# Two sequences' projections as seven quarter products, four passes of two key heads, value pages by indirect transfers

## The chip, the cores and the metric

The kernel runs on one core of a Trainium2 chip, and the metric is the device time of one launch. The core has a matrix engine (TensorE, PE in the profile; PEld is its weight load), VectorE (DVE), ScalarE (ACT), GpSimd (POOL) and SyncE (SP, which here only issues transfers). Each takes its own instructions strictly in the order in which they stand in the program; semaphores order them against each other. Transfers are issued in the queues of SP, ACT and POOL and carried out by 16 DMA engines. Work is done in SBUF, a memory of 128 partitions; TensorE writes to PSUM, eight banks of 512 float32 numbers per partition.

## The reference

Eight sequences of 128 tokens with 512 features pass two residual blocks, all in float32. Block 0 multiplies by one of eight weight matrices per sequence, then by a base matrix with a bias, and adds a low-rank mixture of two of eight experts. Block 1 is attention over a paged cache, followed by a routed low-rank layer:

```python
q = _rope(_rmsnorm(x @ Wq.T, q_norm_w), pos)      # 32 query heads of 128
k = _rope(_rmsnorm(x @ Wk.T, k_norm_w), pos)      # 8 key heads
v = x @ Wv.T
kc = k_cache[block_table].reshape(bsz, 512, 8, 128)   # 16 pages of 32 tokens; vc alike
k_all = concat([kc, k]); v_all = concat([vc, v])      # 640 keys, each head serving 4 query heads
probs = softmax(where(valid, q @ k_all.T * SCALE, -1e30))
o = (probs @ v_all) @ Wo.T
out = x + ((o @ A_w.T).reshape(64, 8) * gate).reshape(512) @ B_w.T * 2
```

`gate` is a softmax over the 16 best of 64 experts. The output is the sequence after both blocks.

## The kernel before

The program is written out by hand: Python loops emit instructions, and each engine keeps the emitted order.

A first stage (lines 269 to 500) makes `x1`, the sequences after block 0, stores them to HBM and keeps them transposed in SBUF as `x1T`. It also loads the first weights of attention and makes the tables of cosines.

The attention stage works in *units*: one sequence and one key head with its four query heads, 64 in all. Units are listed by `units` (line 183) in two passes of four key heads (`GH` = 4): for each of the two halves of heads all eight sequences, and for each sequence four heads. A *step* is one sequence in one pass. `iteration(u)` (line 812) emits, for one value of `u`, pieces of five units:

- the transfers (SP): `gather` (149) loads the next step's key and value pages, one transfer for each page of `kt` and one of `vt`; `exchange_in(u-1)` (708) loads `qkb`, the blocks of rotated queries and keys of unit u+1, and `pT`, the transposed probabilities of unit u-1;
- then for each of four query heads: `scores(u, h)` (650), two matmuls against 512 cached and 128 own keys into a bank pair `s` (two pairs in turn); `mask_exp` (663), a masking pass on VectorE and an exponential on ScalarE; `normalize` of the head before (682), a reciprocal on VectorE and a multiplication on POOL; `blocks` of the head before that (687), a transpose of 32x32 blocks on VectorE into `pb`; and `output(u-2, h)` (751), one matmul of the output projection;
- after the four heads: `add_output(u-2)`, the last `normalize` and two `blocks`, and `exchange_out(u)` (695). That writes `pb`, and with it the queries and keys of unit u+2, to HBM in four transfers `px`, two on SP and two on ACT. Reading them back in another order completes the transpose;
- `project(u+3)`: four matmuls of 512 columns into bank `q` (queries) and four of 256 into bank `kv` (line 201, 214), then `norms` (227), five squares with sums and a copy of the values `vn` on ScalarE and a power on POOL, and `rotate(u+3)` (243) on VectorE;
- `heads_qk(u+1)` (718), a ScalarE copy that makes `qkT` out of `qkb`. The scores of unit u+1 read it;
- `values(u-1)` (727): five matmuls of `pT` with cached and own values, evicted by `evict_o` in the next iteration.

A unit's output of 128x512 is added to the step's sum `ya` on VectorE (line 770) after each unit; between the passes a sum goes to HBM and comes back (`y_d`, `load_y`).

The order within an engine matters for what follows. On ScalarE: four exponentials, two `px` issues (each waits for the last block transpose), five squares and the `vn` copy of unit u+3, the `qkT` copy of unit u+1, then `evict_o` of the next iteration. A transfer issue that waits holds up everything behind it in its engine's queue.

The last stage computes the routed layer. Four of its eight sequences are done within the last iterations (`LAST`, line 777 on), and four after them (`l2`, line 906).

Of the kernel before, what the change touches and what calls it, by code (L numbers as in the profile page):

```python
# [30 lines left out]
GH = HKV // 2  # L31
# [7 lines left out]
WARM = 22  # L39
# [14 lines left out]
def adaln_ffn_kernel(  # L54
# [5 lines left out]
    pages: bass.AP,  # L60
    lens: bass.AP,
# [32 lines left out]
    wp = ctx.enter_context(tc.tile_pool(name="wp", bufs=GH))  # L94
# [5 lines left out]
    pg = const.tile([1, B * NPP], I32, name="pg")  # L100

# [17 lines left out]
    lenf = const.tile([P, B], F32, name="lenf")  # L119
    cos = const.tile([P, B, D // 2], F32, name="cos")  # L120
    sin = const.tile([P, B, D // 2], F32, name="sin")

    x1T = keep.tile([P, B, NC, S], F32, name="x1T")
# [13 lines left out]
    def load_q(g, eng):  # L137
        t = wp.tile([P, NC, (REP + 2) * D], F32, tag="wqkv", name=f"wqkv_{g}")
        eng.dma_start(out=t, in_=wqkv[g].rearrange("(c p) n -> p c n", p=P))
        wq_t[g] = t  # L140

    def load_o(g, eng):
        t = wp.tile([P, REP, DM], F32, tag="wo", name=f"wo_{g}")
        eng.dma_start(out=t, in_=wo[g].rearrange("h p n -> p h n"))
        wo_t[g] = t
# [3 lines left out]
    def gather(step, first=0, end=NPP):  # L149
        hf, b = divmod(step, B)  # L150
        if first == 0:
            kv_t[step] = (
                kvp.tile([P, NPP, GH, PSIZE], F32, tag="kt", name=f"kt_{step}"),
                kvp.tile([P, LC, GH * D], F32, tag="vt", name=f"vt_{step}"),
            )
        kt, vt = kv_t[step]
        per = P // PSIZE
        for j in range(first, end):
# [6 lines left out]
            r0 = (j % per) * PSIZE  # L165
            nc.sync.dma_start(
                out=vt[r0 : r0 + PSIZE, j // per, :],
                in_=vc[hf, ds(page, 1)].rearrange("o p f -> p (o f)"),
# [14 lines left out]
    units = [(st, st // B * GH + j) for st in range(2 * B) for j in range(GH)]  # L183
    NU = len(units)
    q_t, kv_ps, rs_t, qk_t, vn_t, tab_t = {}, {}, {}, {}, {}, {}


    SWAP = (1, 3)
# [12 lines left out]
    def project_q(u):  # L201
        st, g = units[u]
        q = bank("o" if u in SWAP else "q", f"q_{u}")
        for c in range(NC):
            nc.tensor.matmul(  # L205
                out=q,
                lhsT=x1T[:, st % B, c, :],
                rhs=wq_t[g][:, c, : REP * D],
                start=(c == 0),
                stop=(c == NC - 1),  # L210
            )
        q_t[u] = q

    def project_kv(u):
        st, g = units[u]
        kv = bank("y" if u in SWAP else "kv", f"kv_{u}")[:, : 2 * D]
        for c in range(NC):
            nc.tensor.matmul(  # L218
                out=kv,
                lhsT=x1T[:, st % B, c, :],  # L220
                rhs=wq_t[g][:, c, REP * D :],
                start=(c == 0),
                stop=(c == NC - 1),
            )
        kv_ps[u] = kv

    def norms(u):

        q, kv = q_t[u], kv_ps[u]
        ss = pj.tile([P, NH], F32, tag="ss", name=f"ss_{u}", bufs=5)  # L230
        sq = pj.tile([P, D], F32, tag="sq", name=f"sq_{u}")
        for h in range(NH):
            src = q[:, h * D : (h + 1) * D] if h < REP else kv[:, :D]
            nc.scalar.activation(sq, src, AF.Square, accum_out=ss[:, h : h + 1])  # L234
        vn = pj.tile([P, D], F32, tag="vn", name=f"vn_{u}", bufs=5)
        nc.scalar.copy(vn, kv[:, D:])
        vn_t[u] = vn
        nc.gpsimd.tensor_scalar(ss, ss, 1.0 / D, EPS, ALU.mult, ALU.add)  # L238
# [4 lines left out]
    def rotate(u):  # L243

        st, g = units[u]
        q, kv, rs, tab = q_t.pop(u), kv_ps.pop(u), rs_t[u], tab_t[st]
        ca = pj.tile([P, NH, 2, D // 2], F32, tag="ca", name=f"ca_{u}")
        sa = pj.tile([P, NH, 2, D // 2], F32, tag="sa", name=f"sa_{u}")
        for i, o in enumerate((ca, sa)):
            ov = o.rearrange("p h t d -> p h (t d)")  # L250
            tv = tab[:, i].rearrange("p (i t) d -> p i (t d)", t=2)
            nc.vector.tensor_tensor(  # L252
                ov[:, :REP, :],
                q.rearrange("p (h d) -> p h d", h=REP),
                tv[:, 0:1, :].to_broadcast([P, REP, D]),
                ALU.mult,
            )
        for i, o in enumerate((ca, sa)):
# [3 lines left out]
                ov[:, REP, :], kv[:, :D], rs[:, REP:NH], tv[:, 1, :], ALU.mult, ALU.mult  # L262
# [6 lines left out]
    with ExitStack() as l0:  # L269
# [30 lines left out]
        homes = [(p2, "wt"), (p2, "wt"), (wp, "wo"), (kvp, "kt"), (kvp, "vt"), (wp, "wqkv")]  # L300
        wt_home = {}

        def l0_home(b):
            pool, tag = homes[b if b < 5 else b - 5 if b < 7 else 5]
            n = (REP + 2) * D if tag == "wqkv" else DM
            t = pool.tile([P, NC, n], F32, tag=tag, name=f"wt_{b}")
            wt_home[b] = t[:, :, :DM]

        for b in (0, 1, 2, 3, 4, 7):
            l0_home(b)  # L310
# [26 lines left out]
        )  # L337
        leni = w0p.tile([P, B], I32, name="leni")
# [102 lines left out]
        def l0_experts(b):  # L441
# [5 lines left out]
            state[b] = x1  # L447

        def l0_turn(b):
# [4 lines left out]
            nc.scalar.copy(x1T[:, b].rearrange("p c s -> p (c s)"), tp[:, :DM])  # L454
# [5 lines left out]
        for t in range(B):  # L460
# [4 lines left out]
            if t + 3 < B:  # L465
                if t + 3 in (5, 6):
                    l0_home(t + 3)
# [3 lines left out]
            if t >= 1:  # L471
                l0_experts(t - 1)
                if t in (3, 5, 7):
                    load_q((t - 3) // 2, nc.gpsimd)
# [6 lines left out]
            l0_base(t)  # L481
            if 1 <= t <= 4:
                l0_angles(t - 1)

        load_q(3, nc.gpsimd)
        for g in range(GH):
            load_o(g, nc.gpsimd)
        make_tables(0)
        project_q(0)
        l0_turn_low(B - 1)  # L490
        project_kv(0)
        norms(0)
        l0_experts(B - 1)
        l0_turn(B - 2)
        rotate(0)
        project_q(1)
        l0_turn(B - 1)
        project_kv(1)
        norms(1)
        rotate(1)  # L500
# [4 lines left out]
    def f_weights():  # L505
        awt = wp.tile([P, NC, (REP + 2) * D], F32, tag="wqkv", name="awt")
        nc.sync.dma_start(
            out=awt[:, :, :DM], in_=aw.rearrange("(c p) n -> p c n", p=P)
        )
        bwt = wp.tile([P, NC, (REP + 2) * D], F32, tag="wqkv", name="bwt")  # L510
        nc.sync.dma_start(
            out=bwt[:, :, :DM], in_=bw.rearrange("(c p) n -> p c n", p=P)
        )
        nc.sync.dma_start(
            out=awt[:RD, :, DM : DM + P], in_=wr.rearrange("r (c p) -> r c p", p=P)
        )
        nc.sync.dma_start(out=awt[:RD, 0, DM + P : DM + P + E1], in_=keys)
        fw_t["a"], fw_t["b"] = awt[:, :, :DM], bwt[:, :, :DM]
        fw_t["s"] = bwt[:, :, DM : DM + E1]
        fw_t["r"], fw_t["k"] = awt[:RD, :, DM : DM + P], awt[:RD, 0, DM + P : DM + P + E1]  # L520
# [10 lines left out]
    def f_turn(b, sb, psum):  # L531
        yb = ya_t.pop(B + b)
# [59 lines left out]

    ORDER = [B - 3, B - 2, 0, 1, 2, B - 1, 3, 4]
# [11 lines left out]
    with ExitStack() as l1:  # L605
# [145 lines left out]
        def output(u, h):  # L751
            st, g = units[u]
            if h == 0:
                y_t[u] = bank("y", f"y_{u}")
            nc.tensor.matmul(  # L755
                out=y_t[u],
                lhsT=oT_t[u][:, h, :],
                rhs=wo_t[g][:, h, :],
                start=(h == 0),
                stop=(h == REP - 1),  # L760
            )

        def add_output(u):
            st, g = units[u]
            y = y_t.pop(u)
            if g == 0:
                ya_t[st] = yp.tile([P, DM], F32, tag="ya", name=f"ya_{st}")
                nc.vector.tensor_copy(ya_t[st], y)
            else:
                nc.vector.tensor_tensor(ya_t[st], y, ya_t[st], ALU.add)  # L770
            if g % GH == GH - 1 and st < 2 * B - 3:
                nc.sync.dma_start(out=y_d[st % B], in_=ya_t.pop(st))
            del oT_t[u]
# [3 lines left out]
        LAST = {NU - 3: B - 3, NU - 2: B - 2, NU - 1: 0, NU: 1}  # L777
        rooms, yT_t = {}, {}

        def room(b):  # L780
            small = b < B - 3
            w = wp.tile(
                [P, REP * DM if small else NC * (REP + 2) * D],
                F32,
                tag="wo" if small else "wqkv",
                name=f"room_{b}",
            )
# [274 lines left out]
```

## Time and profile before

Three runs took 1275.34, 1275.35 and 1276.76 us; the median is 1275.35. The profile is of one further execution, whose own time was 1278.66 us, with a span (first to last instruction) of 1276.9.

| From the profile | |
|---|---|
| granted TensorE clock | 0.996 |
| TensorE busy | 1260.5 us, 99% |
| VectorE, ScalarE, GpSimd busy | 61%, 36%, 27% |
| DMA queue of SP: packets, MB, share of 16 engines | 153,044, 218.83, 53.7% |
| DMA queue of ACT | 18,960, 52.21, 12.0% |
| DMA queue of POOL | 4,464, 21.14, 4.8% |
| first and last values matmul (line 734) start | 125.5 us, 1219.2 us |

In a row of groups, "x512" is the number of instructions, then come the busy time in us, the mean duration in ns, and the idle time of that engine before them with what ended it. A float32 matmul is two instructions (passes); their spans overlap in the profile, so the distance between starts says what one costs. In the timeline each line is start, duration, engine, source line, operation, and what it writes and reads. ACTq and SPq are the issues of transfers in those queues.

### The profile page before, as it was taken

How to read it: one execution, taken by the hardware profiler on the slowest of the kernel's cores; microseconds unless marked ns; L12 is line 12 of the kernel's file. 1: busy time of each engine (PE TensorE's matmuls, PEld its weight loads, DVE VectorE, ACT ScalarE, POOL GpSimd, SP SyncE). 2: the span in 40 equal slices, each digit the busy share in tenths (PEclk: the TensorE clock that was granted, in tenths of full speed). 3: DMA queues.
4: the chain of work that ended last, by engine and by line, in shares of the span. 5: the costliest groups of instructions: out<-in, count | busy, mean ns of one | idle time of the engine just before them, and what ended most of it. 6: DMA issues, size and time to landing. Idle time of an engine off the chain costs nothing.

```text
span 1276.9 us, 15242 instructions
## 1 busy us (share of the span) xinstructions
PE 1260.5 (99%) x3949; PEld 671.8 (53%) x3949; DVE 781.8 (61%) x1794; ACT 465.7 (36%) x1397; POOL 342.1 (27%) x462
## 2 busy tenths in 40 slices
PE   8999999999999999999998999999999999999998
PEld 6765555555555555544554455555555555555554
DVE  2437766666666666666665666666666666665524
ACT  0225344334434433434333344334344334433211
POOL 2134232323223222323232232322232223221100
PEclk9999999999999999999999999999999999999999
DMA  9885677686768666799888676776777676786531
GB/s 313 304 291 162 205 230 234 198 246 211 235 207 260 213 222 227 229 309 294 267 272 273 202 247 207 243 230 218 234 229 238 201 256 213 234 273 217 179 109 49
DMA packets 176555, 293.15 MB, mean 230 GB/s; under 512 B 15971, under 2 KB 85924, under 8 KB 176468
## 3 DMA queue, kind: packets, MB, share of 16 engines
q1 hardware_dynamic: 153044, 218.83, 53.7%
q10 hardware_dynamic: 18960, 52.21, 12.0%
q0 software_dynamic: 4464, 21.14, 4.8%
q8 instruction: 31, 0.51, 0.2%
q14 instruction: 56, 0.46, 0.1%
HBM read 180.64 MB, written 111.48 MB: 229 GB/s over the span
## 4 chain that ended last, share of the span: by engine, by line
PE 91%; DMA 6%; DVE 1%; issue 0%; SPq 0%; ACT 0%; POOL 0%; ACTq 0%; DVEq 0%
PE o L734 21%; PE s L655 16%; PE y L755 16%; PE q L205 15%; PE kv L218 8%; PE s L658 4%; DMA pT<-px 4%; PE cp L379 2%; PE op L957 2%; PE bp L401 2%; DMA px<-pb 2%; PE fz L552 1%; PE fp L552 1%; PE cp L396 1%; PE bp L443 1%; DMA wt<-in_w 0%
## 5 line engine op out<-in xcount | busy, mean ns | idle before, releaser
L685 POOL TENSOR_SCALAR p<-p,den 128x640 f32<-128x640 f32 x256 | 204.4, 798 | 523.9 <-DVE den L684 523.8
L679 ACT ACTIVATE p<-p,low 128x640 f32<-128x640 f32 x256 | 212.2, 829 | 325.7 <-DVE den L684 230.9
L668 DVE CUSTOM_DVE_ANT_0 p<-s,mask,rs 128x640 f32<-128x640 f32 x256 | 226.1, 883 | 161.3 <-PE s L658 149.8
L755 PE MATMUL y<-wo,oT 128*128 128x512 f32 x512 | 261.4, 594 | 0.3 <-ACT oT L745 0.3
L655 PE MATMUL s<-kt,qkT 128*128 128x512 f32 x512 | 261.7, 593 | 0.0
L734 PE MATMUL o<-pT,vt 128*128 128x512 f32 x512 | 233.6, 599 | 7.9 <-DMA pT<-px 5.3
L205 PE MATMUL q<-wqkv,x1T 128*128 128x512 f32 x512 | 230.2, 592 | 0.0
L690 DVE STREAM_TRANSPOSE pb<-p 128x640 f32<-128x640 f32 x256 | 210.9, 824 | 11.8 <-POOL p L685 11.7
L658 PEld LDWEIGHTS s<-qkT 128*128 128x128 f32 x512 | 97.3, 190 | 122.4 <-issue 122.4
L205 PEld LDWEIGHTS q<-wqkv,x1T 128*128 128x128 f32 x512 | 97.0, 190 | 120.5 <-issue 120.5
L655 PEld LDWEIGHTS s<-kt,qkT 128*128 128x128 f32 x512 | 96.8, 190 | 119.0 <-issue 102.9
L734 PEld LDWEIGHTS o<-pT,vt 128*128 128x128 f32 x512 | 97.8, 192 | 108.4 <-issue 95.4
L234 ACT ACTIVATE sq<-q 128x128 f32<-128x128 f32 x256 | 71.0, 277 | 215.4 <-DVE pb L690 102.2
L252 DVE TENSOR_TENSOR ca<-q,tab 128x512 f32<-128x512 f32 x64 | 44.1, 690 | 168.4 <-ACT sq L234 163.3
L218 PE MATMUL kv<-wqkv,x1T 128*128 128x256 f32 x512 | 121.0, 379 | 0.0
L218 PEld LDWEIGHTS kv<-wqkv,x1T 128*128 128x128 f32 x512 | 97.0, 190 | 38.9 <-issue 29.0
L658 PE MATMUL s<-qkT 128*128 128x128 f32 x512 | 98.4, 274 | 0.0
L238 POOL TENSOR_SCALAR ss<-ss 128x5 f32<-128x5 f32 x64 | 12.6, 197 | 266.6 <-ACT sq L234 266.6
L745 ACT COPY oT<-o 128x512 f32<-128x512 f32 x64 | 37.5, 585 | 119.6 <-PE o L734 119.6
L755 PEld LDWEIGHTS y<-wo,oT 128*128 128x128 f32 x512 | 78.2, 192 | 3.6 <-issue 2.9
L240 POOL TENSOR_TENSOR rs<-ss,mhalf 128x5 f32<-128x5 f32 x64 | 75.4, 1179 | 5.3
L734 PE MATMUL o<-pT,vn 128*128 128x512 f32 x128 | 65.4, 592 | 0.0
(145 smaller groups left out, 954.5 us busy)
## 6 DMA issues: line engine op xcount, KB each, us to landing
pT<-px SPq DMA_DIRECT2D x64, 1280.0 KB, 6.8
px<-pb SPq DMA_DIRECT2D x122, 400.0 KB, 5.3
px<-pb ACTq DMA_DIRECT2D x122, 400.0 KB, 5.1
qkb<-px SPq DMA_DIRECT2D x61, 320.0 KB, 3.4
kt<-in_kc SPq DMA_DIRECT2D x256, 64.0 KB, 5.2
vt<-in_vc SPq DMA_DIRECT2D x256, 64.0 KB, 4.5
wqkv<-in_wqkv POOLq DMA_DIRECT2D x8, 1536.0 KB, 8.3
wo<-in_wo POOLq DMA_DIRECT2D x8, 1024.0 KB, 11.2
```

The costliest lines, as they stand in the source:

```text
L205: nc.tensor.matmul(out=q, lhsT=x1T[:, st % B, c, :], rhs=wq_t[g][:, c, : REP * D], start=(c == 0), stop=(c == NC - 1),)
L218: nc.tensor.matmul(out=kv, lhsT=x1T[:, st % B, c, :], rhs=wq_t[g][:, c, REP * D :], start=(c == 0), stop=(c == NC - 1),)
L234: nc.scalar.activation(sq, src, AF.Square, accum_out=ss[:, h : h + 1])
L240: nc.gpsimd.tensor_tensor(rs, ss, mhalf, ALU.pow)
L655: nc.tensor.matmul(out=s[:, :L], lhsT=qkT[:, h, :], rhs=kt[:, :, g % GH, :], start=True, stop=True)
L658: nc.tensor.matmul(out=s[:, L:NK], lhsT=qkT[:, h, :], rhs=qkT[:, REP, :], start=True, stop=True)
L668: nc.vector.tensor_tensor_reduce(out=p, in0=s_t.pop((u, h))[:, :NK], in1=mask_t[st], scale=rs_t[u][:, h : h + 1], scalar=BIG, op0=ALU.add, ...
L679: nc.scalar.activation(p, p, AF.Exp, bias=low, scale=-1.0, accum_out=den)
L685: nc.gpsimd.tensor_scalar(p_t[u, h], p_t[u, h], den, 1.0, ALU.mult, ALU.mult)
L690: nc.vector.transpose(pb_t[u][:, :, h * w : (h + 1) * w].rearrange("p i (j a) -> p j i a", a=32), p_t.pop((u, h)).rearrange("p (j i a) -> ...
L734: nc.tensor.matmul(out=o, lhsT=vt[:, c, j * D : (j + 1) * D] if c < LC else vn_t.pop(u), rhs=pT[:, c], start=(c == 0), stop=(c == LC),)
L755: nc.tensor.matmul(out=y_t[u], lhsT=oT_t[u][:, h, :], rhs=wo_t[g][:, h, :], start=(h == 0), stop=(h == REP - 1),)
```

## The change

**Products.** The two sequences of a pair (2p, 2p+1) are projected together. The stacked input has two row blocks (sequences) and two column blocks (halves of the 512 features); the weights of a head have two row blocks and two column blocks of `HW` = 384 (two query heads and the key; two query heads and the value). The 2x2 block product is formed with seven block products in place of eight. Four input sums and four weight sums precede them, made on POOL (`sums_x`, `sums_q`); the products' results are combined by VectorE adds from PSUM into `c0` and `c1`, tiles in SBUF for the two sequences. Squares, `vn` and the rotation now read these instead of PSUM.

To keep float32 rounding alike for both sequences, each row of `x1` is scaled by a power of two before its transposition; `vn` is scaled back, and the norm's epsilon is scaled with it.

**Order.** Products of later units are emitted one by one inside the head loop, after heads 1, 2 and 3; where `four` holds (u odd) a fourth comes after the rotation.

**Passes.** `GH` is 2: four passes of two key heads, 32 steps. The output of a step's two units is summed in one PSUM bank, and one add per step remains; `y` goes to HBM and back three times. Key pages are loaded in halves of 256 B per partition. Six of the eight sequences of the routed layer are done within the last iterations.

**Value pages.** `gather_v` loads 128 rows of 1 KB per transfer, with row numbers from a table `vrow`, as indirect transfers in POOL's queue; `gather` on SP loads keys alone.

**Start.** 36 idle transposes instead of 22; two weight loads in the first stage instead of four.

```diff
-GH = HKV // 2
+GH = 2
+NQ = HKV // GH
+HW = NH // 2 * D + D
-WARM = 22
+WARM = 36
...
+    def sums_q(g, first):
+        w = wq_t[g]
+        if first:
+            nc.gpsimd.tensor_tensor(w[:, 5], w[:, 3], w[:, 1], ALU.subtract)
+            nc.gpsimd.tensor_tensor(w[:, 1], w[:, 1], w[:, 0], ALU.subtract)
+        else:
+            nc.gpsimd.tensor_tensor(w[:, 4], w[:, 3], w[:, 1], ALU.subtract)
+            nc.gpsimd.tensor_tensor(w[:, 6], w[:, 2], w[:, 4], ALU.subtract)
...
-            nc.sync.dma_start(
-                out=vt[r0 : r0 + PSIZE, j // per, :],
-                in_=vc[hf, ds(page, 1)].rearrange("o p f -> p (o f)"),
-            )
+    def gather_v(step, first=0, end=LC):
+        hf, b = divmod(step, B)
+        for c in range(first, end):
+            at = b * LC + c
+            nc.gpsimd.indirect_dma_start(
+                out=kv_t[step][1][:, c, :], out_offset=None, in_=vc,
+                in_offset=bass.IndirectOffsetOnAxis(ap=vrow[:, hf, at : at + 1], axis=0),
+            )
...
+    PRODUCTS = {
+        1: (0, 0, "q"), 2: (1, 2, "kv"), 3: (6, 3, "q"), 4: (3, 6, "q"),
+        5: (2, 1, "kv"), 6: (4, 4, "q"), 7: (5, 5, "kv"),
+    }
+    def project(k, j, products):
+        pr, g = k % (B // 2), k // (B // 2) * GH + j
+        key = k, j
+        for i in products:
+            x, y, tag = PRODUCTS[i]
+            ps = bank(tag, f"p_{k}_{j}_{i}")[:, :HW]
+            w = wq_t[g][:, y].rearrange("p (c n) -> p c n", c=2)
+            for c in range(2):
+                nc.tensor.matmul(
+                    out=ps, lhsT=xo[:, pr, x, c, :], rhs=w[:, c, :], start=(c == 0), stop=(c == 1)
+                )
+            add = lambda out, a: nc.vector.tensor_tensor(out, a, ps, ALU.add)
+            if i == 1:
+                ...
+                nc.scalar.copy(part_t[key], ps)
+            u, c0, c1 = part_t[key], c_t[4 * k + j], c_t[4 * k + 2 + j]
+            if i == 2:
+                add(c0[:, :HW], u)
+            elif i == 6:
+                add(u, u)
+            elif i == 7:
+                add(c1[:, HW:], u)
+            elif i == 4:
+                add(c1[:, :HW], c1[:, HW:])
+            elif i == 5:
+                add(c1[:, HW:], c1[:, HW:])
+                add(c0[:, HW:], u)
+            elif i == 3:
+                add(c0[:, HW:], c0[:, HW:])
...
         def iteration(u):
+            slots = ()
+            if u > 1 and k < NU // 4:
+                slots = (1, 2, 6) if four else (4, 5, 3)
...
+            if pages:
+                gather(st + 1, first, first + 3)
             if on(u - 1):
                 exchange_in(u - 1)
+            if pages:
+                gather(st + 1, first + 3, first + NPP // GH)
+            if pages:
+                gather_v(st + 1, u % GH * LC // GH, (u % GH + 1) * LC // GH)
+            if u % GH == 0 and B <= st - 1 < NQ * B:
+                load_y(st - 1)
...
             for h in range(REP):
                 if on(u):
                     scores(u, h)
                     mask_exp(u, h)
...
                 if on(u - 2):
                     output(u - 2, h)
+                if h > 0 and slots:
+                    project(k, j, slots[h - 1 : h])
             if on(u - 2):
                 add_output(u - 2)
+            if on(u + 1) and (u + 1) % GH == 0:
                 make_mask(units[u + 1][0])
             if on(u):
                 normalize(u, REP - 1)
                 blocks(u, REP - 2)
                 blocks(u, REP - 1)
                 exchange_out(u)
...
-                project(u + 3)
+                norms(u + 3)
                 rotate(u + 3)
+                if four and (slots or u == 1):
+                    project(k, j, (7,))
             if u + 1 in range(3, NU):
                 heads_qk(u + 1)
+            if slots and k % 4 == 3 and k < NU // 4 - 1 and not four:
+                load_q((k // 4 + 1) * GH + j, nc.gpsimd)
+            if u > 8 and u < NU - 8 and u % 16 in (9, 10, 11, 12):
+                sums_q((u // 16 + 1) * GH + u % 16 // 11, u % 16 in (9, 11))
...
             if on(u - 1):
                 values(u - 1)
```

## The prediction

> **What bounds the kernel now.** I read the page first: engine shares, then the chain that ended last, then the groups.
>
> ```profile
> span 1276.9 us, 15242 instructions
> ...
> PE 1260.5 (99%) x3949; PEld 671.8 (53%) x3949; DVE 781.8 (61%) x1794; ACT 465.7 (36%) x1397; POOL 342.1 (27%) x462
> ...
> PE 91%; DMA 6%; DVE 1%; issue 0%; SPq 0%; ACT 0%; POOL 0%; ACTq 0%; DVEq 0%
> ...
> L234 ACT ACTIVATE sq<-q 128x128 f32<-128x128 f32 x256 | 71.0, 277 | 215.4 <-DVE pb L690 102.2
> ```
>
> TensorE is the bound: its row has no idle time worth naming. Its cost per unit comes from the chain in order of time: eight passes of 512 columns take 3.43 us, 0.429 each. A unit is four times (scores 0.86 + 0.22, output 0.86) = 7.76, projection 3.43 + 1.73 = 5.16, values 4.29; together 17.21, and consecutive units do start 17.21 us apart. So a shorter projection pays only while nothing else needs 17.21 us per unit. The last row above names the candidate: ScalarE's squares wait for `pb`, the transposed probabilities, which they do not read. The timeline of one unit (first score at 792.82) shows why.
>
> ```profile
> 792.82 1.02 PE L655 MATMUL s<-kt,qkT 128*128 128x512 f32 x2
> ...
> 799.50 0.38 PE L658 MATMUL s<-qkT 128*128 128x128 f32 x2
> ...
> 800.56 0.88 DVE L668 CUSTOM_DVE_ANT_0 p<-s,mask,rs 128x640 f32<-128x640 f32 x1
> ...
> 802.20 0.65 DVE L770 TENSOR_TENSOR ya<-y,ya 128x512 f32<-128x512 f32 x1
> ...
> 802.77 0.14 DVE L684 RECIPROCAL den<-den 128x1 f32<-128x1 f32 x1
> ...
> 803.01 0.80 POOL L685 TENSOR_SCALAR p<-p,den 128x640 f32<-128x640 f32 x1 [0.58 <-DVE den L684]
> ...
> 803.84 0.84 DVE L690 STREAM_TRANSPOSE pb<-p 128x640 f32<-128x640 f32 x1 [0.18 <-POOL p L685]
> ...
> 804.72 0.85 ACTq L702 DMA_DIRECT2D px<-pb  x2
> 805.67 0.28 ACT L234 ACTIVATE sq<-q 128x128 f32<-128x128 f32 x1 [3.20 <-DVE pb L690]
> ...
> 807.68 0.74 ACT L721 COPY qkT<-qkb 128x640 f32<-128x640 f32 x1
> ...
> 810.03 1.02 PE L655 MATMUL s<-kt,qkT 128*128 128x512 f32 x2
> ```
>
> Fourth score ends 7.06 us after the first began (call the end T). The last transpose ends T + 4.80. Only then can ScalarE issue the two `px` transfers in its queue; behind them stand five squares, the `vn` copy and the `qkT` copy, which ends 3.70 after the issue, and the next unit's first score needs that `qkT`. A loop from score to score: 7.06 + 4.80 + 0.04 + 3.70 = 15.60, slack 1.61 in most units, 1.16 where a mask is made in between. In the one unit where TensorE followed the copy and its period stretched to 17.30, the gap was 0.32: the latency of this wait. The loop is hidden by 1.3 us only.
>
> [...]
>
> **The change, part by part.**
>
> *Products.* The built program has 448 projection matmuls of 384 columns in place of 256 of 512 and 256 of 256: columns per unit 3072 to 2688. A product (four passes of 384, 0.322 each) is 1.29; TensorE saves 0.65 per unit, 41 us in all, if it stays the bound.
>
> *Where they stand.* Before, the projection came after the fourth score. Now three products sit in the head loop, behind heads 1, 2 and 3, so two of them, 2.58 us, lie between the first and the fourth score: T moves from 7.06 to 9.64. That alone exceeds the slack. A fourth product (odd units) precedes the values and is off this loop.
>
> *VectorE.* Seven adds of 128x384 (0.56 each, from 0.69 for 512) and a ScalarE copy per two units evict them. The third product ends at T + 2.15 (output 0.86, product 1.29), and its add is queued before the reciprocal of the last head, where VectorE waits for it. Even units: add at T + 2.2, reciprocal T + 2.69, then as in the trace 0.24, 0.83 and 0.84 for POOL and the transpose: `px` at T + 4.65. Odd units also have the `ya` add (0.57 from start to next start) and the next mask (0.45, the slack difference above) there: T + 5.67. The `ya` add is halved in number, but leaves even units only, where the product's add has its place.
>
> *ScalarE.* Squares and `vn` now read SBUF[...]: `px` to `qkT` 3.97.
>
> *Per unit.* Even: 9.64 + 4.65 + 3.97 + 0.32 = 18.58; odd 19.60; mean 19.09 against 17.21, +1.88. TensorE's own need is 15.92 and 17.21, so it idles in every unit. Units 2 to 58 have products: 57 x 1.88 = +107 us.
>
> *POOL.* Weight differences: two operations on 128x768 in each of 12 units; 256 elements take 0.76, 512 take 1.27, so 1.8 each, 3.6 a unit, ahead of the next normalizations: estimated +6 us in all. Two gathers per unit, 1.1 each assumed (bounds 0.8, the direct load, and 3): POOL is 27% busy, and the first normalization has 2.9 us to spare in odd units (VectorE transposes `ca` first). Cost nothing here.
>
> *DMA.* Key pages stay at eight issues a unit on SP; their packets go from 512 B to 256 B and double; value pages leave SP for POOL's queue; 16 more loads and 11 more stores of `y`. The 16 engines were 74% busy in mid-span; the longer unit makes room. `pT`, issued 0.95 after `px` has landed (7.0) and landing 6.8 later, comes at 29.0 (even) and 30.1 (odd) after the first score; the values that read it start in the next unit, at 31.5 and 31.2. Hidden by 1 to 2.5 us; late landings cost more than before, inside the range.
>
> *Start.* Before the first values matmul TensorE does 25 products (32.2) against five projections (25.8): +6. Three waits are new there, from the order of VectorE and ScalarE: the third score of unit 0 behind the rotation of unit 1 (about 4), `tq` of unit 2 behind a rotation whose squares stand behind `px` (4), a product whose bank is freed behind another rotation (8). The 14 extra idle transposes (0.21 each) fill a 2.6 us wait for `wt`. +25 us, bounds 10 and 35.
>
> *End.* Two of four final feed-forward sequences move from the tail (4.4 us of TensorE each) into units that idle: -9.
>
> Sum against the profiled execution: 1276.9 + 107 + 6 + 25 - 9 = 1406; the runs' median is 1.5 below that span: 1404.
>
> **Rivals.** (1) TensorE stays the bound: 1276.9 - 41, about 1235. For it speak 99% and 91%; it needs the loop to be shorter than 15.92 and 17.21, 2.4 to 2.7 us less than worked out, as if the squares and `vn` (2.5 us) did not stand ahead of the `qkT` copy. The built order has them there. Below 17.2 in the mean it would not be slower. (2) The gathers become the bound: from about 2.5 us each, every further microsecond costs two per unit; at 3 us each, +62, about 1466. Against it: POOL's direct loads take 0.82. (3) A milder loop: adds and start-up partly hidden, periods near 18.2, 57 x 1.0 + 20, about 1345. (4) That fewer columns are not computed at all is excluded by the counts above. (5) `pT` late in many units: +20, inside the likeliest case's width.
>
> **How the numbers follow.** Likeliest case, the score-to-score loop, 0.70, 1375 to 1435; (2) 0.12, above; (3) 0.13, below; (1) 0.04; no change 0.01. Leaving half of (3), half of (2) and (1) outside gives 1350 to 1455. About 0.2% (2.5 us) is what these runs can tell from no change. Faster 0.04, same 0.01, slower 0.95.
>
> **What would show it.** Right: TensorE about 88% busy, its largest idle row the first score waiting for `qkT`; periods alternating near 18.6 and 19.6; `px` issued 14.3 and 15.3 us after the first score. Wrong: idle rows before the values waiting for `pT`, or normalizations waiting behind gathers; a period near 17; a gather well over 1.1 us.

## The result, and the profile after

The changed kernel takes 1454.86 us (four runs, 1452.31 to 1458.24) against 1276.05 us of the kernel before (four runs, 1275.34 to 1277.83): 1.140 times as long, 95% interval 1.137 to 1.143. Slower, as forecast, but by 179 us instead of 128: the time lies at the very upper end of the range. The profiled execution has a span of 1453.7 us. From the page, by parts 1, 4 and 5:

```profile
span 1453.7 us, 15896 instructions
...
PE 1294.0 (89%) x3835; PEld 666.5 (46%) x3835; DVE 916.4 (63%) x2049; ACT 495.3 (34%) x1437; POOL 579.9 (40%) x683
...
PE 57%; DVE 15%; ACT 12%; POOL 7%; issue 4%; ACTq 3%; DMA 1%; SPq 1%; POOLq 0%; DVEq 0%
...
L742 PE MATMUL s<-kt,qkT 128*128 128x512 f32 x512 | 291.9, 654 | 128.5 <-ACT qkT L808 113.9
...
L289 ACT ACTIVATE sq<-c 128x128 f32<-128x128 f32 x320 | 99.0, 309 | 258.6 <-DVE pb L777 229.3
```

TensorE is no longer the bound: 89% busy, and its largest idle row is the first score waiting for `qkT`. The chain now runs through VectorE, ScalarE and POOL too. One thing does not fit: 448 projection matmuls of 384 columns are less work than before, yet TensorE is busy for 33.5 us longer. Its mean granted clock is 0.959, where it was 0.996.

The timeline of an even unit, with the columns of the prediction's second fence:

```profile
758.26 1.12 PE L742 MATMUL s<-kt,qkT 128*128 128x512 f32 x2 [1.94 <-ACT qkT L808]
...
767.63 0.39 PE L745 MATMUL s<-qkT 128*128 128x128 f32 x2
...
770.20 0.55 DVE L261 TENSOR_TENSOR c<-c,p 128x384 f32<-128x384 f32 x1 [0.42 <-PE p L258]
770.67 0.16 DVE L771 RECIPROCAL den<-den 128x1 f32<-128x1 f32 x1
770.92 0.80 POOL L772 TENSOR_SCALAR p<-p,den 128x640 f32<-128x640 f32 x1 [0.99 <-DVE den L771]
771.75 0.84 DVE L777 STREAM_TRANSPOSE pb<-p 128x640 f32<-128x640 f32 x1 [0.18 <-POOL p L772]
...
772.63 0.84 ACTq L789 DMA_DIRECT2D px<-pb  x2
773.52 0.31 ACT L289 ACTIVATE sq<-c 128x128 f32<-128x128 f32 x1 [3.54 <-DVE pb L777]
...
775.85 0.71 ACT L808 COPY qkT<-qkb 128x640 f32<-128x640 f32 x1
...
776.62 1.12 PE L742 MATMUL s<-kt,qkT 128*128 128x512 f32 x2 [2.16 <-ACT qkT L808]
```

This is the predicted loop, step by step: the fourth score ends 9.75 us after the first began, the third product's add stands before the last reciprocal, `px` is issued 14.4 us after the first score, the squares stand behind it (ScalarE idles 3.54 us ahead of the first, put down to `pb`, which the squares do not read), and the next score follows the `qkT` copy by 0.05 us. The period is 18.36.

But many units take 20.04 and 21.11 us in place of 18.35 and 19.42. In all of these the whole difference lies between the first and the fourth score: 11.44 us instead of 9.75. The windows view shows why. Its columns are the stretch, its length, the busy time of the five engines, the granted clock, the DMA share and the rate:

```profile
494.97:498.38 3.41, 1.25 (x4) 0.57 (x4) 0.31 (x2) 2.70 (x11) 1.62 (x3) 1.00 1.02 336
498.38:501.80 3.42, 3.42 (x7) 1.60 (x6) 2.00 (x6) 0.92 (x2) 3.09 (x4) 0.50 0.60 183
501.80:505.21 3.41, 3.41 (x12) 1.79 (x11) 0.97 (x3) 1.40 (x3) 1.08 (x2) 1.00 0.92 307
...
774.90:778.31 3.41, 1.70 (x6) 0.98 (x7) 0.93 (x3) 2.11 (x7) 2.31 (x3) 1.00 1.01 315
778.31:781.73 3.42, 3.42 (x12) 1.83 (x11) 2.35 (x7) 1.72 (x4) 2.94 (x3) 1.00 0.91 252
```

In the first stretch of 3.41 us TensorE idles for 2.16, and through the next one it has half its clock, which costs 1.7 us of work. In the fourth it idles for 1.71 and nothing follows. The half-clock stretches lie on a fixed grid of 3.41 us: all 34 of this trace start on it, within 0.01 us. In units 3 to 57, all 16 grid stretches with 2.08 us or more of idle time were followed by one; of 13 with 1.93 to 2.00 us, 11 were; of those with 1.90 or less, none. A wait of 2.16 us is enough here if it falls into one stretch of this grid.

The wait for `qkT` alternates between 1.94 and 2.16 us as the trace counts it. Whether a wait lies inside one stretch of the grid depends on the phase, and the phase holds itself: a unit with a half-clock stretch takes 20.57 in the mean, which is nearly six of the 3.41 us stretches (20.48). From 457.4 to 580.3 us seven stretches follow each other at 20.48 us, and from 815.8 to 979.7 us nine. That the period holds the phase is read from this trace; no run was made to test it.

The difference of the two spans, 176.8 us, by places (units counted from the start of their first score):

| | us |
|---|---|
| 55 units (3 to 57), loop at full clock: mean of 18.35 and 19.42 less 17.21 | +92.1 |
| half clock in 26 of these units | +44.4 |
| units with weight sums and the one after each group (13.0), and others | +14.3 |
| transfers that were late in the kernel before, with the half clock behind one of them; not a loss of the change | -8.9 |
| start, up to unit 3 | +34.8 |
| end, from unit 58 | -0.4 |

They add to 176.3; the rest is rounding of the periods. Over the whole span the half-clock stretches take 58.3 us of work from TensorE, and 4.5 in the kernel before; that more than accounts for the 33.5 us by which its busy time rose with less to do. The second and the third row overlap: some stretches lie in units that the weight sums hold up in any case (see the first experiment).

### The profile page after: what moved, and what is told of

It reads as the page before. It is cut to its first block, busy times and chain, and to the rows that moved or that the text cites. A ratio compares the mean times of both kernels' runs of the same rounds, so it can differ in the third digit from the quotient of the medians.

```text
span 1453.7 us, 15896 instructions
## 1 busy us (share of the span) xinstructions
PE 1294.0 (89%) x3835; PEld 666.5 (46%) x3835; DVE 916.4 (63%) x2049; ACT 495.3 (34%) x1437; POOL 579.9 (40%) x683
## 4 chain that ended last, share of the span: by engine, by line
PE 57%; DVE 15%; ACT 12%; POOL 7%; issue 4%; ACTq 3%; DMA 1%; SPq 1%; POOLq 0%; DVEq 0%
PE p L258 16%; PE s L742 15%; PE y L843 14%; ACT sq L289 8%; DVE pb L777 4%; PE s L745 4%; POOL p L772 3%; ACTq L789 3%; PE o L821 2%; PE op L1080 2%; ACT qkT L808 2%; DVE ca L317 2%; DVE c L261 2%; DVE sa L317 2%; POOL rs L295 1%
## 5 line engine op out<-in xcount | busy, mean ns | idle before, releaser
L742 PE MATMUL s<-kt,qkT 128*128 128x512 f32 x512 | 291.9, 654 | 128.5 <-ACT qkT L808 113.9
L258 PE MATMUL p<-wqkv,xo 128*128 128x384 f32 x896 | 322.9, 491 | 5.8 <-DVE c L261 5.8
L843 PE MATMUL y<-wo,oT 128*128 128x512 f32 x512 | 285.0, 643 | 3.7 <-ACT oT L832 3.7
L258 PEld LDWEIGHTS p<-wqkv,xo 128*128 128x128 f32 x896 | 171.3, 192 | 161.8 <-issue 80.5
L289 ACT ACTIVATE sq<-c 128x128 f32<-128x128 f32 x320 | 99.0, 309 | 258.6 <-DVE pb L777 229.3
L317 DVE SCALAR_TENSOR_TENSOR ca<-c,rs,tab 128x128 f32<-128x128 f32 x64 | 43.0, 672 | 224.9 <-POOL rs L295 224.9
L203 POOL DMA_INDIRECT vt<-in_vc,vrow x128 | 134.0, 1047 | 32.8 <-issue 32.6
L293 POOL TENSOR_SCALAR ss<-ss,eps 128x5 f32<-128x5 f32 x64 | 17.4, 271 | 260.6 <-ACT sq L289 260.6
L261 DVE TENSOR_TENSOR c<-c,p 128x384 f32<-128x384 f32 x96 | 51.9, 541 | 34.5 <-PE p L258 34.4
L289 ACT ACTIVATION_READ_ACCUMULATOR sq<-c 128x1 f32 x320 | 59.6, 186 | 0.0
```

The source lines that it names most:

```text
L203: nc.gpsimd.indirect_dma_start(out=kv_t[step][1][:, c, :], out_offset=None, in_=vc, in_offset=bass.IndirectOffsetOnAxis(ap=vrow[:, hf, at ...
L258: nc.tensor.matmul(out=ps, lhsT=xo[:, pr, x, c, :], rhs=w[:, c, :], start=(c == 0), stop=(c == 1))
L289: nc.scalar.activation(sq, cs[:, at : at + D], AF.Square, accum_out=ss[:, h : h + 1])
L317: nc.vector.scalar_tensor_tensor(ov[:, REP, :], cs[:, 2 * D : HW], rs[:, REP:NH], tv[:, 1, :], ALU.mult, ALU.mult)
L742: nc.tensor.matmul(out=s[:, :L], lhsT=qkT[:, h, :], rhs=kt[:, :, g % GH, :], start=True, stop=True)
L843: nc.tensor.matmul(out=y_t[st], lhsT=oT_t[u][:, h, :], rhs=wo_t[g][:, h, :], start=(h == 0 and j == 0), stop=(h == REP - 1 and j == GH - 1),)
```

## The experiments

Theory: the score-to-score loop sets the period, and idle TensorE time then costs clock as well. Rivals: the clock falls for another reason; something other than the scores sets the pace; the page transfers do. Twelve kernels were run, each edited from the changed kernel or from the run named. Most times are single ones, and are compared where differences are over 10 us. One kernel below that was run four times spread over 10 us, so steps of 12 to 18 us between single times are weak by themselves; what their traces show beside them counts for more.

**Filling the wait.** The products' bank is free there, and nothing reads the result.

```diff
             if on(u - 1):
                 values(u - 1)
+            if 2 <= u < NU - 6:
+                idle = bank("q", f"idle_{u}")
+                for i in range(8):
+                    nc.tensor.transpose(idle[:, :S], ident, ident)
```

> The changed kernel with eight idle transposes of 128 columns (0.21 us each, 1.7 us together) put on TensorE behind the values of each unit from 2 to 57, where it otherwise waits 2.2 to 2.4 us for qkT. They compute nothing that is used. In the changed kernel every stretch of 3.41 us that held 2.08 us or more of TensorE idle time was followed by 3.41 us at half clock. Theory that idle time itself takes the clock away: the wait shrinks to 0.5 to 0.7 us, no half-clock stretch is left between units 3 and 57 (26 before, 44 us together), the score-to-score periods are 18.35 and 19.42 throughout but for the weight-sum units, and the time falls by about 44 us to 1411. Rival, the clock falls for another reason (the mixture of work, the mean load): the stretches stay and the time stays near 1455, or rises by what the transposes take.

1418.27 us, 37 less, with 448 more instructions on TensorE. Between units 3 and 57 one half-clock stretch is left, where 26 units had one; the median periods are 18.36 and 19.42. The mean clock is 0.989. The same 100 us in the windows view, first of the changed kernel, then of this one (the clock is the third number from the end):

```profile
480.00:580.00 100.00, 89.63 (x235) 44.12 (x234) 60.61 (x134) 36.32 (x107) 34.85 (x43) 0.93 0.62 198
```

```profile
480.00:580.00 100.00, 93.99 (x298) 49.69 (x297) 66.88 (x148) 38.09 (x112) 39.57 (x49) 1.00 0.66 210
```

More work on TensorE made the kernel faster: the idle time takes the clock. The gain is 37 us and not 44 because not every stretch had set its unit's length. In unit 11 the stretch stays. In units 27, 42 and 43, which have weight sums, it is gone, and the unit takes as long as with it (within 0.1 us): the sums hold it up anyway. So the clock's price in the units is 37 to 38 us. The twelve units with sums and the three behind them take 21.5 us more than others in both kernels, with five stretches (8.5 us) in the changed one and one (1.7) here: the sums' own part is 13.0 us by the first count, as in the table, and 19.8 by the second.

**One product less between the scores.** The first product of the next unit goes behind the values of this one.

```diff
-                if h > 0 and slots:
-                    project(k, j, slots[h - 1 : h])
+                if slots and h in {2: 1, 3: 2}:
+                    project(k, j, slots[{2: 1, 3: 2}[h] : {2: 1, 3: 2}[h] + 1])
...
                 values(u - 1)
+            k2, j2, _, next_slots = planned(u + 1)
+            if next_slots:
+                project(k2, j2, next_slots[:1])
```

> The changed kernel with one of the three products of each head loop emitted one slot earlier: the first of them behind the values of the unit before, so in the wait for qkT, and the others after heads 2 and 3, so that one product instead of two stands between the first and the fourth score. Theory of the score-to-score loop: first to fourth score 8.46 us instead of 9.75, everything behind it unchanged, periods 17.06 and 18.13 instead of 18.35 and 19.42, TensorE idle about 1.1 us a unit, so no half-clock stretches: 55 x 1.29 + 44 = 115 us less, about 1340. Rival, the period is held by something that does not start from the scores (a transfer, ScalarE's or VectorE's own load): the first to the fourth score shortens but the period does not, and the time stays above 1410.

1382.75 us. First to fourth score: 8.46 in odd units, as worked out, and 8.83 in even ones, where the third score now waits for the first mask, which VectorE has queued behind the rotation. Median periods 17.44 and 18.14 for 17.06 and 18.13 expected; from the fourth score on all is as before (4.62 and 5.68 to `px`, 3.94 to `qkT`). So the period starts from the scores. The time is 43 us above the expected 1340. The rest of the miss lies mostly in the units with weight sums and their neighbours, which take up to 24.5 us: there the first normalization stands on POOL behind sums, gathers and tables without a pause between them. Seven half-clock stretches (12 us) are left there and behind a wait for `pT`; none was expected.

**Squares ahead of `px`.**

```diff
                 blocks(u, REP - 1)
+                if u > 1 and on(u + 3):
+                    norms(u + 3)
                 exchange_out(u)
...
-                norms(u + 3)
+                if u == 1:
+                    norms(u + 3)
                 rotate(u + 3)
```

> The changed kernel with the five squares, vn and the power of unit u+3 emitted before the px transfers of unit u instead of behind them, nothing else. Theory of the loop: the squares and vn (2.3 us between the px issue and the qkT copy) leave the loop, which comes to about 16.05 and 17.12 us, against TensorE's own 15.92 and 17.21; TensorE is the bound again or nearly, and no half-clock stretches are left. 55 x 2.2 + 44 = 165 us less, 1290, if nothing else is late; pT, which lands 29 to 30 us after the first score, is then late for the values in odd units by up to 1.3 us, so 1290 to 1325, with new idle time of the values waiting for pT. Rival, the squares' place does not matter because the px transfers and what follows them set the pace: 1410 or more.

1336.12 us, 119 less, just above the expected range. From the `px` issue to the `qkT` copy 1.61 us instead of 3.93, and the next score no longer follows the copy. What took over was named, but its size was not: the values wait for `pT`. The chain and the row of the values:

```profile
PE 57%; DMA 28%; DVE 5%; POOL 3%; issue 3%; SPq 1%; ACT 1%; ACTq 1%; POOLq 0%; DVEq 0%
...
L821 PE MATMUL o<-pT,vt 128*128 128x512 f32 x512 | 243.6, 620 | 57.0 <-DMA pT<-px 56.9
```

Transfers, 1% of the chain in the changed kernel, hold 28% here. Five half-clock stretches are left between units 3 and 57, each behind a wait of 2.6 to 3.4 us for `pT`; none was expected.

**Value pages in SP's queue again.**

```diff
-            nc.gpsimd.indirect_dma_start(
-                out=kv_t[step][1][:, c, :],
...
-                in_offset=bass.IndirectOffsetOnAxis(ap=vrow[:, hf, at : at + 1], axis=0),
-            )
...
+            page = nc.sync.value_load(pg[0:1, at : at + 1])
...
+            nc.sync.dma_start(
+                out=kv_t[step][1][r0 : r0 + PSIZE, j // per, :],
+                in_=pages_v[hf, ds(page, 1)].rearrange("o t f -> (o t) f"),
+            )
```

> The changed kernel with the value pages loaded page by page in SP's queue as in the kernel before (16 transfers of 32 rows a step), in place of four indirect transfers a step in POOL's queue; the other parts stay. The prediction took the indirect transfers as costing nothing, which would also mean that they gain nothing if the queue that they left has room: then 1455 within 5 us. Rival: with steps of two units SP has 16 page issues a unit at 0.74 us each, 11.8 us, besides qkb, pT and px (2.0 us) and a wait of 5 to 7 us for px to land, together about 19 us against a period of 18.9: SP then holds up px and pT, idle time of the values waiting for pT or vt appears, and the time is 1470 to 1500.

1584.66 us, 130 more than with indirect transfers, and 85 above the range that the rival gave. Its largest waits of TensorE and of its weight loads (engine, line, what ended the wait: total, times, longest):

```profile
PEld o L822 <- DMA pT<-px: 187.9, 51, 11.3
...
PE o L822 <- DMA pT<-px: 174.5, 51, 10.7
```

SP issues sixteen pages a unit at 0.74 to 0.9 us each, then `px` stands behind them and `pT` behind `px`. The clock falls to 0.930: between units 3 and 57 half clock takes 85 us, where it took 44, so up to 41 of the 130 us are clock. At these steps the indirect transfers are a part of the change that gains: 1.05 us each on POOL (134.0 us for 128), hidden, against a queue that would be the bound. Steps of two units have twice the page issues per unit that steps of four had; what indirect transfers are worth with four was not run.

**Products behind the fourth score, as the projection was.**

```diff
-                if h > 0 and slots:
-                    project(k, j, slots[h - 1 : h])
...
             elif on(u + 3):
+                if slots:
+                    project(k, j, slots)
                 norms(u + 3)
```

> The changed kernel with its three products of a unit put back to where the projection stood before: behind the fourth score and the px issues, ahead of the squares; no product in the head loop. By the score-to-score loop alone the first to fourth score takes 7.06 us again, qkT comes 15.7 and 16.8 us after the first score, TensorE is the bound, and the time is near 1260. Rival, worked out from the banks: two banks serve the products in turn, so the third waits for the eviction of the first, and that eviction now stands on VectorE behind the last block transposes (4.6 us after the fourth score) or on ScalarE behind the px issues: third product at about 5.2 to 6 us after the fourth score, in place of 3.4, and the squares and values behind it; periods of 18 and 20, about 1400 to 1430, with TensorE idle before the products.

1465.11 us. First to fourth score 7.06, as before, but periods of 17.8 and 22.4. Two of the largest waits of TensorE:

```profile
PE p L258 <- ACT u L264: 97.5, 28, 6.5
...
PE p L258 <- DVE c L261: 52.1, 31, 4.7
```

The rival holds, and is stronger than worked out: the copy of the first product stands behind `px` on ScalarE, and the bank that it frees is the third product's. With two banks this place is no better than the slots in the head loop, which lengthen the loop; whether a third bank would free it was not tried.

**Towards TensorE's own time.** The next kernels add to each other. First, on the kernel with the squares ahead: `pT` before `qkb`, and all key pages behind both.

```diff
-            if pages:
-                gather(st + 1, first, first + 3)
             if on(u - 1):
                 exchange_in(u - 1)
             if pages:
-                gather(st + 1, first + 3, first + NPP // GH)
+                gather(st + 1, first, first + NPP // GH)
```

> The kernel with the norms first, and in SP's queue pT is loaded first, then qkb, then all the key pages, in place of three pages, qkb, pT, five pages. Theory: with the squares out of the loop the values wait for pT (57 us of TensorE idle time), and pT is late because three page issues (up to 4.3 us) and qkb stand before it; issued 1 to 1.5 us earlier and with less traffic ahead of it, most of those waits go: 1336 less 35 to 55, so 1280 to 1300. Rival, pT is late because its 1.28 MB take 7 us on loaded engines, whatever the order: 1320 or more.

1353.17 us, 17 more: wrong. Part 6 of its page (issues, KB, us to landing):

```profile
px<-pb SPq DMA_DIRECT2D x122, 400.0 KB, 7.4
px<-pb ACTq DMA_DIRECT2D x122, 400.0 KB, 4.4
```

The half of `px` that goes through SP's queue now follows eight key pages there, where it followed five, and takes 3.0 us longer to land than ScalarE's half; in the changed kernel the two took 5.3 and 6.3. `pT` needs both. From ScalarE's last `px` issue to the first transfer that reads `px` 9.2 us pass in the median, against 7.4 in the kernel with the squares ahead; the next two runs, which keep the eight pages there, have 8.2 and 8.6, and the one that goes back to five has 7.1. The place of the pages was never changed alone, so their part is likely and not isolated.

> The kernel before this one in the list, with two more moves: the ya add and the mask behind the px issues in the order of VectorE (in odd units they put px off by 1.06 us), and the eight weight-sum operations one by one behind the normalizations of heads 0 and 1 of four units, in place of two together ahead of a unit's gathers (in the changed kernel the units with sums and the one after them took 14 us more than the others). Theory: px of odd units comes 1.06 us earlier and the sums vanish from the path: 10 to 20 us less than the run before, 1265 to 1285. Rival: TensorE is already the bound between the two and only the sums' part is to be had: 0 to 10 us less.

1340.96, 12.2 less than the run before. In 11 of the 28 odd units from 3 to 57 `px` is now issued as early as in even ones, 4.6 us after the fourth score; in the others it is not, and the median of odd units is 5.25, where it was 5.79. The step was of the expected size, from a start that had been put too low.

> The kernel before this one in the list, with the order of the start changed too: rotation of unit 1 behind the first two masks of unit 0, squares of units 2 and 3 inside unit 0, and the products of unit pairs 2 to 5 spread over the head loops of units 0 and 1. The three waits named in the prediction for the start measured 4.79, 5.74 and 4.95 us in the changed kernel, and half-clock stretches lie behind them. Theory: two thirds of these 15.5 us go, and some of the half-clock time: 10 to 16 us less than the run before, about 1255 to 1270, which would be below the kernel before. Rival: the products of the start are themselves the bound and the waits only move: 0 to 4 us less.

1324.56, 16.4 less. 11.1 of it lies before unit 3, whose first score comes at 168.8 us instead of 179.9.

> The kernel with the changed start, in which the values wait for pT (79 us of TensorE and weight-load idle time in the trace), with SP's order back to three pages, qkb, pT, five pages (all eight pages behind pT had made the px transfers of SP slower, 7.4 us to land against 4.4 on ScalarE's queue, which was the fault of that idea), and with more room for pT: the first product of the next unit moves ahead of the values of this one, the products take their two banks strictly in turn, and the sums wait one unit longer for their weights. px is issued 1.29 us earlier and the values stay where they are in the unit. Theory: pT's lateness is the last thing between this kernel and TensorE's own 15.9 and 17.2 us a unit; with 1.3 us more room most of it goes: 1324 less 30 to 50, 1275 to 1295. Rival: the transfers take what they take, and only the waits move: 1310 or more.

1306.53, 18 less for an expected 30 to 50. `px` is issued 13.0 us after the first score in both kinds of units (8.35 and 4.62), and most units run at TensorE's 15.92 and 17.21. The ten largest waits of the values that are left take 2.5 to 5.6 us each; nine of them stand in the unit right after one in which weights are loaded.

> The kernel of the run before in the list, with pT ahead of qkb in SP's queue (three pages, pT, qkb, five pages). Theory: pT lands up to 1 us earlier, and where the values still wait this goes: 5 to 20 us less than the run before, 1260 to 1285. Rival: pT and qkb share the engines whatever their order, and nothing changes; or qkb becomes late for qkT, and it is slower by as much.

1288.72 us (four runs, 1281.0 to 1290.98), 1.010 times the kernel before, 1.007 to 1.013. That is 18 less than the single time of the run before, as much as expected, from a start that had been put too low again.

> The kernel of the run before in the list, with all four px transfers of a unit issued in ScalarE's queue, so that none stands behind key pages in SP's. Theory: px lands in 4.4 us on both halves, pT is issued 1 to 2 us earlier, and the last waits for pT go: 5 to 15 us less than the run before. Against it: ScalarE spends 0.85 us more a unit on issues ahead of the qkT copy, and the first score waits for that: 5 to 15 us more.

1388.28 us, 100 more. Its timeline on ScalarE:

```profile
722.32 4.30 ACTq L795 DMA_DIRECT2D px<-pb  x4
726.67 0.72 ACT L815 COPY qkT<-qkb 128x640 f32<-128x640 f32 x1 [4.70 <-DVE c L267]
```

Two such issues took 0.84 us in this queue in the changed kernel; these four take 4.30. From the first `px` issue to the end of the `qkT` copy 4.9 us (even) and 5.8 (odd) pass in the median instead of 1.6, and the score-to-score loop is back at 18.8 and 19.3. The price in the expectation (0.85 more) came from two issues and did not hold for four.

**Weight loads in parts**, on the kernel of the last but one run:

```diff
+    def load_q_part(g, i):
+        if i == 0:
+            wq_t[g] = wp.tile([P, 7, 2 * HW], F32, tag="wqkv", name=f"wqkv_{g}", bufs=GH)
+        nc.gpsimd.dma_start(
+            out=wq_t[g][:, i].rearrange("p (c n) -> p c n", c=2),
+            in_=wqkv[g, i].rearrange("(c p) n -> p c n", p=P),
+        )
...
+        PARTS = {
+            (8, 4): ("q", 0, 0), (9, 0): ("q", 0, 1), (9, 1): ("q", 0, 3), (9, 3): ("q", 0, 2),
...
                         normalize(u, h - 1)
+                    weights(u, h)
```

> The kernel with pT ahead of qkb in SP's queue, and its last waits taken up: in the trace of that kernel TensorE waits 23.3 us for pT in 13 units, and each of these but one comes in the unit after a whole load of weights (1.5 MB of projection weights, 1 MB of output weights, in POOL's queue); the longest, 4.9 us, follows 2 MB of the last layer's weights issued in SP's queue just ahead of pT. Five half-clock stretches follow these waits (8.5 us). Here each weight load is cut into four parts that are issued one at a time over two to three units, the last layer's weights go to POOL's queue in parts of 256 KB, and the products of unit 1 stand one head earlier (a wait of 5.0 us for the transposes of unit 2). Theory: most of 23 + 8 us of waits and lost clock go, and part of the 5: 1289 less 15 to 30, 1259 to 1274, below the kernel before. Rival: the same bytes in the same stretch of time make pT as late as before: 1280 or more.

1255.87 us (five runs, 1254.08 to 1261.02): 0.984 times the kernel before, 0.981 to 0.987, so faster than both, and a little below the expected range. The edit joins several moves (parts, queue, place of a product), whose shares were not told apart. The waits for `pT` in the kernel before this edit and in this one:

```profile
PE o L828 <- DMA pT<-px: 23.3, 13, 4.9
```

```profile
PE o L845 <- DMA pT<-px: 8.9, 9, 1.9
```

No half-clock stretch is left between units 3 and 57. TensorE is 98% busy over a span of 1254.1, with 1224.7 us of work against 1260.5 in the kernel before. The 35.8 us are near the 41 that the shorter products should save: their gain, seen at last.

## Why the prediction was right or wrong

- **The score-to-score loop: right, but for the latency.** First to fourth score 9.64 predicted, 9.75 measured; to `px` 4.65 and 5.67, measured 4.62 and 5.68; `px` to `qkT` 3.97, measured 3.93; latency 0.32, measured 0.05. Of the 3.97, 0.27 was the author's estimate for reading SBUF; a square took 309 ns from SBUF, and 277 from PSUM in the kernel before. Periods 18.58 and 19.60, measured 18.35 and 19.42 at full clock. `gap1` and `norms_first` moved it where it should move. The loop's term of 107 for 57 units is 92 for 55.
- **The clock: missing from the sum.** That TensorE "idles in every unit" was written down and given no price. It costs 44.4 us in the units, and 8.9 at the start and 5.1 at the end more. This is the step that failed: the prediction put idle TensorE time at the length of the wait alone. `fill` takes 37 us of the units' part away. The profile of the kernel before had an example: its one long wait in the loop, 3.42 us for `pT`, brought 6.8 us of half clock at 698.4 us:

```profile
699.62 6.45 PE L734 MATMUL o<-pT,vt 128*128 128x512 f32 x8 [3.42 <-DMA pT<-px]
```

- **Weight sums: mis-sized.** +6 predicted, without a sum behind it; 13.0 measured in the twelve units with sums and the three behind them, lost clock put apart, and 19.8 in `fill`, where hardly any clock is lost.
- **Start: right places, too small a sum.** The three waits measured 4.79, 5.74 and 4.95, 15.5 together for 16 predicted; that the sum fits is luck in part, since 4, 4 and 8 stood there. With 6 of more products and 7 of half clock beyond the kernel before, 6 of the 34.8 us stay unexplained; predicted were 25, bound 35.
- **End: no gain.** -9 predicted, -0.4 measured; three half-clock stretches (5.1) lie there. What took the other 3.5 was not followed up.
- **Gathers at no cost: right.** 1.1 each was the author's assumption, 1.05 was measured. What they are worth against page transfers in SP's queue, 130 us at this step size, was not asked.
- **`pT` in time: right.** The values waited 4.7 us for it in all. Its small margin (1 to 2.5 us) showed when the loop became shorter: 57 us of waits in `norms_first`.
- **The range: met by luck.** Its upper part, up to 1455, was there for slow gathers and a late `pT`. Neither came; lost clock, start and weight sums filled that room.
- **Rivals.** That TensorE stays the bound named the right condition, squares not ahead of the `qkT` copy; with that alone the time is 1336, not 1235, as the transfers come next. The milder loop and the slow gathers did not happen.

## What to carry to other kernels

When an edit lets a matrix engine that was always busy wait a little in every turn of a loop, price the lost clock beside the wait (here 44.4 us in 26 of 55 units), and ask how the period stands to the grid on which the half-clock stretches lie in its trace (here 20.57 us to six times 3.41). Work that moves between two steps of a loop lengthens it even where it fills an idle engine (here the first to the fourth score went from 7.06 to 9.75 us): look for what is queued behind the issue that waits. When the bound moves away, the next one (here the transfers of `pT`, 57 us of waits in `norms_first`) appears at once, so a part of a change that seems free can be what holds it up.

## What the runs showed of the hardware that was not expected

- On a grid of 3.41 us, in units 3 to 57 of the changed kernel, half clock (1.7 us of work lost each time) followed all 16 stretches with 2.08 us or more of idle TensorE time, 11 of 13 with 1.93 to 2.00 us, and none with 1.90 or less. Where the period came near six stretches (20.57 us against 20.48), up to nine half-clock stretches followed each other at that distance.
- Two `px` issues of 400 KB took 0.84 us in ScalarE's queue, four took 4.30.
- `px` took 7.4 us to land in SP's queue with eight key pages issued right before it, and 5.3 in the changed kernel with five; the two kernels differ in more than that.
